# Mixer loop: decay sums placed between the outputs in both directions, step sizes computed inside the wait for the sums of squares, normalization scaled during the states

## The chip, the cores and the metric

The program runs on one core of a Trainium2 chip. The metric is device time in microseconds (us) of one execution; the kernel before has a median of 1464.55 us over three runs (1463.51 to 1469.52). A core has a matrix engine (PE), which also loads weights (PEld), a vector engine (DVE), an activation engine (ACT), a general engine (POOL) and a queue of DMA issues (SP). Each engine works through its own instructions in order; engines wait for each other by semaphores.

## The reference

Everything is float32. A batch of 8 images of 32x32 positions and 128 channels is read as 8 sequences of 1024 tokens. Layer 0 adds an attention over the tokens. Layer 1 adds a mixer, which is a state-space model run once forwards and once backwards over the tokens, and then adds a spectral filter. Only the mixer is touched by the change. Cut to its core it is:

```python
def mamba(x, in_proj, conv_w, conv_b, A_log, dt_bias, D, norm_w, out_proj):
    z, xbc, dt = split(x @ in_proj)                  # 256, 256 + 64 + 64, 4 columns
    xbc = silu(causal_conv(xbc, conv_w) + conv_b)    # 4 taps along the tokens
    xh, Bm, Cm = split(xbc)
    dt = softplus(dt + dt_bias)                      # one step size for token and head
    dA = dt * -exp(A_log)
    # per chunk of 64 tokens, cs = cumsum(dA)
    L = exp(cs_l - cs_s) for s <= l                  # decays inside the chunk
    y_in = (Cm @ Bm.T * L) @ (xh * dt)
    states = Bm.T @ (exp(cs_last - cs) * xh * dt)    # one state for a chunk and head
    prev = scan(states, exp(cs_last))                # 15 steps from chunk to chunk
    y = y_in + (Cm @ prev) * exp(cs) + xh * D
    y = y * silu(z)
    return (y * rsqrt(mean(y * y) + 1e-5) * norm_w) @ out_proj
t = layer_norm(x)
x = x + mamba(t, forward weights) + reverse(mamba(reverse(t), backward weights))
```

## The kernel before

The attention runs first, to about 456 us. The mixer follows, to about 1057 us, and the spectral filter takes the rest. The mixer has 16 units, one for each sequence and direction (`Unit(b, d)`, with d = 0 forwards and d = 1 backwards), in the order (0,0), (0,1), (1,0) and so on. One pass of the loop at L1258 finishes the recurrence of unit `u`, prepares the one after it (`following`) and closes the one before it (`last`). So three units are in flight. The order of instructions on every engine, SP included, is the order in which the Python code issues them (`manual_schedule(engines=ALL_IN_ORDER)`, L1220); nothing reorders them later. `behind(t, other)` adds a dependency by hand.

In what follows a forward pass is a pass whose `u` has d = 0, and a backward pass one whose `u` has d = 1. A forward pass also brings the tokens of the next sequence in (`fresh`): `turn_tokens` transposes them, `steps` makes the step sizes. A backward pass also normalizes the sequence after that (`normalize`, `normalized`).

What the steps do, with their tiles:

- `add_decays(u)` (L853): PE multiplies `da` with triangles into the PSUM tile `pdec`, ACT copies two results out (`cums`, `dsum`). `turn_decays(u)` (L868): one PE transpose of `cums` into the same `pdec`, one ACT copy (`cs`). `take_decays(u)` (L874): ACT takes exponentials (`cums`, `rest`, `dec`), SP stores them and loads them back spread over partitions (`lm`, `ec`).
- `from_row` (L903): POOL computes `cs - lm`, held `behind` the second convolution tap. `between` (L913): ACT applies Relu, and one pass later Exp, to the two halves of `lm`. `weigh_decays` (L1101): DVE multiplies `lm` by the products of B and C (`gm`, half of the tile `bg`).
- `project_x`, `copy_x`, `first_tap`, `convolve`, `activate_x`: projection (`pp`), copy (`xp`), first tap on ACT (`xs`, L954), three taps for each of two halves on DVE (L962), Silu on ACT (L967). `project_z` and `activate_z`: the gate (`pz`, `zs`, L975). `project_bc` and `activate_bc`: B and C (`pb`, then `bt` and `ct`, L1000).
- `turn_x` (L1005): 16 transposes on PE (`sx`), times the step size on DVE (`xdt`, L1016). `turn_b`: `sb`, copied by ACT to `bg` (L1038). `weigh_start` (L918): POOL multiplies `ec` by `ct`, held behind the last tap.
- `chunk_states` (`pst`) on PE, `pass_states` (L1080, L1083) on DVE, whose results SP copies to the other partitions (`moved`). `outputs` (`sy`, L1131): 248 small products in two halves.
- `end(last)` (L1228): the output projection `spo` and the sums of squares (`misc`, L1174), which ACT copies out (L1182), PE transposes (L1188), DVE scales (`rms_v`, L1190) and POOL raises to the power -0.5 (`rms`, L1192). `scale_rows` (L1196) multiplies `spo` by it on ACT; `add_rows` (L1202) adds to `X` on DVE.
- `steps` (L478): 8 small products (`pd`), three DVE instructions (`sp_v`, `sp_e`), Exp on ACT, one on DVE (`sp_u`), Ln on ACT, four on DVE. It is a generator, which the loop advances from `yield` to `yield`.
- `rsqrt` (L129): a POOL multiply-add (`ln_r_v`) and a POOL power (`ln_r`). In the mixer it is held behind the second tap.

PSUM has two pools here, each with two slots of 128x1024: `ps_w` (`sx`, `sb`, `px`, `pp`, `pd`, `pz`, `pb`, `pdec`) and `ps_s` (`spo`, `misc`, `pst`, `sy`). A tile gets a slot when the last reader of an earlier tile is done with it. In one pass `ps_s` is used in the order `spo`, `misc`, `pst`, `pst`, `sy`, `sy`; so the first `pst` waits for `scale_rows`, the last reader of `spo`.

Of the kernel before, what the change touches and what calls it, by code (L numbers as in the profile page):

```python
# [45 lines left out]
def fast_kernel(ctx: ExitStack, tc: tile.TileContext, a: dict, out: bass.AP, bad: bass.AP):  # L46
# [80 lines left out]
    begun = []  # L127

    def rsqrt(pool, src, n, scale, eps, name):  # L129

        t = pool.tile([P, n], F32, tag=name + "_v", name=name + "_v")
        begun.append(nc.gpsimd.tensor_scalar(t, src, scale, eps, ALU.mult, ALU.add))
        r = pool.tile([P, n], F32, tag=name, name=name)
        nc.gpsimd.tensor_tensor(r, t, mhalf.to_broadcast([P, n]), ALU.pow)
        return r
# [308 lines left out]
    def normalize(pool, b, later=False):  # L444
        st = pool.tile([P, NT, 6], F32, tag="ln_st", name=f"b_st{b}")
        mv = pool.tile([P, NT, 2], F32, tag="ln_mv", name=f"b_mv{b}")
        for j in range(NT):
            nc.vector.bn_stats(st[:, j, :], X[b][:, j, :])  # L448
        for j in range(NT):
            nc.vector.bn_aggr(mv[:, j, :], st[:, j, :])  # L450
        return mv, None if later else rsqrt(pool, mv[:, :, 1], NT, 1.0, 1e-5, "ln_r")
# [26 lines left out]
    def steps(b, seq, pd):  # L478
# [13 lines left out]
        for j in range(NT):  # L492
            nc.tensor.matmul(
                pd[:, j, :],
                lhsT=xt[:, pad + j * P : pad + (j + 1) * P],
                rhs=wdt.rearrange("p d h -> p (d h)"),
                start=True,
                stop=True,
            )
        v = small("sp_v")  # L500
# [3 lines left out]
        nc.vector.tensor_tensor(e, e, v, ALU.min)  # L504
        nc.scalar.activation(e, e, AF.Exp)
# [81 lines left out]
    with ExitStack() as s:  # L587
# [182 lines left out]
        for n in range(len(units) + 2):  # L770
# [35 lines left out]
            elif n == 117:  # L806
                sizes = steps(0, seqs[0], ps_t.tile([P, T], F32, tag="t", name="pd0"))
                next(sizes)
# [12 lines left out]
    with ExitStack() as s:  # L821
# [91 lines left out]
        def between(u, function, scale):  # L913

            for half in u.lm.rearrange("p (i h) j l -> i p (h j l)", i=2):
# [312 lines left out]
        def end(u, pool):  # L1228
# [5 lines left out]
            project_out(u, range(4, 6))  # L1234
            turn_sums(u, misc)
            project_out(u, range(6, 8))
# [9 lines left out]
        turn_decays(units[1])  # L1246
# [11 lines left out]
        for at, u in enumerate(units[:-1]):  # L1258
# [4 lines left out]
            early_decays = after_it and u.d == 1  # L1263
            if u.d == 1:
                turn_decays(following)
# [3 lines left out]
            between(u, AF.Exp, -1.0)  # L1269
# [5 lines left out]
            if fresh:  # L1275
                turn_tokens(fresh, seqs[fresh], wide_psum(ps_w, f"px{fresh}"))
            project_x(following, 0)
# [6 lines left out]
            if early_decays:  # L1284
                add_decays(after_it)
            causal(u)
            decayed_x(u)
            weigh_decays(u, 0)
            if last:
                end(last, ps_s)  # L1290
            if early_decays:
                turn_decays(after_it)
            first_tap(following, 0)
            if last:
# [4 lines left out]
            if u.d == 1 or u.b == B - 1:  # L1299
                norm = normalize(bridge, b, later=True)  # L1300
            going = iter(())
            if fresh:
                going = steps(fresh, seqs[fresh], wide_psum(ps_w, f"pd{fresh}"))
                next(going)
            weigh_decays(u, 1)
            convolve(following, 0, range(pad - 1))
            next(going, None)
# [4 lines left out]
            if norm:  # L1312
                mv = norm[0]
                norm = mv, rsqrt(bridge, mv[:, :, 1], NT, 1.0, 1e-5, "ln_r")
                behind(begun[-1], following.convolved, "beside the states")
            from_row(following, following.convolved)
            chunk_states(u)
            pass_states(u)
            next(going, None)
            norming = normalized(b, bridge, *norm) if u.d else iter(())  # L1320
            next(norming, None)
# [5 lines left out]
            between(following, AF.Relu, 1.0)  # L1327
# [4 lines left out]
            if after_it and not early_decays:  # L1332
                add_decays(after_it)
            activate_x(following, 1)
            next(norming, None)
# [1104 lines left out]
```

## Time and profile before

| | us |
|---|---|
| median of three runs | 1464.55 |
| the profiled execution | 1462.86 |
| its span, first to last instruction | 1461.1 |
| mixer, first `sx` of the first unit to first `sx` of the last | 533.4 |
| a forward pass, first `xdt` to first `xdt` of the next pass, as from 835.05 to 872.77 | 37.7 |
| a backward pass, as from 872.77 to 906.97 | 34.2 |

The times of a pass are read from the timeline of DVE: the first product with the step sizes (`xdt`, L1016) opens a pass, since it follows the first eight transposes. A row of the timeline gives the start, the duration, engine, line, operation and tiles (out<-in); in brackets stands how long the engine was idle before, and what released it. A row of the waits gives who waited for whom, the total in us, how often, and the longest. "issue" is a wait for which the profile shows no instruction.

### The profile page before, as it was taken

How to read it: one execution, taken by the hardware profiler on the slowest of the kernel's cores; microseconds unless marked ns; L12 is line 12 of the kernel's file. 1: busy time of each engine (PE TensorE's matmuls, PEld its weight loads, DVE VectorE, ACT ScalarE, POOL GpSimd, SP SyncE). 2: the span in 40 equal slices, each digit the busy share in tenths (PEclk: the TensorE clock that was granted, in tenths of full speed). 3: DMA queues.
4: the chain of work that ended last, by engine and by line, in shares of the span. 5: the costliest groups of instructions: out<-in, count | busy, mean ns of one | idle time of the engine just before them, and what ended most of it. 6: DMA issues, size and time to landing. Idle time of an engine off the chain costs nothing. (4 is left out here: it accounts for less than half of the span.)

```text
span 1461.1 us, 45273 instructions
## 1 busy us (share of the span) xinstructions
PE 1336.9 (91%) x19782; PEld 838.2 (57%) x19782; DVE 1094.3 (75%) x2138; ACT 912.1 (62%) x1421; POOL 504.1 (34%) x510
## 2 busy tenths in 40 slices
PE   5999999999998888999898898999789899999977
PEld 2223333333333566666666565656679899999963
DVE  5689889788777687878787878788555577777745
ACT  2666666766766777777777777776355455555520
POOL 3326966885400332323232323233276111111100
PEclk9999999999999999999999999999889999999989
DMA  7101111110002333433433343443269322322258
GB/s 181 36 1 30 45 37 37 42 46 23 8 1 59 73 74 86 91 88 88 89 88 88 89 90 86 100 92 71 73 193 240 110 69 78 85 69 76 69 147 322
DMA packets 139382, 123.09 MB, mean 84 GB/s; under 512 B 44808, under 2 KB 118152, under 8 KB 135080
## 3 DMA queue, kind: packets, MB, share of 16 engines
q1 hardware_dynamic: 137064, 115.93, 31.1%
q8 instruction: 157, 2.57, 0.8%
q10 hardware_dynamic: 2112, 4.19, 0.8%
q14 instruction: 49, 0.40, 0.1%
HBM read 78.15 MB, written 34.08 MB: 77 GB/s over the span
## 5 line engine op out<-in xcount | busy, mean ns | idle before, releaser
L692 ACT ACTIVATE pr<-pt 128x1024 f32<-128x1024 f32 x256 | 248.1, 1021 | 115.6 <-PE pt L687 114.1
L717 DVE TENSOR_TENSOR two<-pr,pr 128x1024 f32<-128x1024 f32 x128 | 162.8, 1312 | 19.8 <-ACT pr L692 18.9
L1514 ACT COPY gs<-pg 128x512 f32<-128x512 f32 x256 | 132.6, 603 | 63.8 <-PE pg L1501 47.9
L1512 DVE COPY gs<-pg 128x512 f32<-128x512 f32 x256 | 158.7, 682 | 14.6 <-PE pg L1501 9.6
L687 PE MATMUL pt<-q,k 32*128 32x512 f32 x1024 | 159.0, 650 | 7.0 <-ACT pr L692 4.7
L1501 PE MATMUL pg<-taps,mst 32*128 32x128 f32 x4096 | 146.0, 281 | 4.2 <-ACT gs L1514 3.4
L1501 PEld LDWEIGHTS pg<-taps,mst 32*128 32x128 f32 x4096 | 134.0, 189 | 16.4 <-issue 11.6
L708 PE MATMUL po<-pr,v 128*32 128x512 f32 x1024 | 141.2, 607 | 0.0
L1535 PE MATMUL py<-gs,u 128*32 128x128 f32 (+1 forms) x4096 | 127.8, 277 | 0.0
L984 PE MATMUL pb<-bxt,wbc 128*128 128x512 f32 x256 | 113.9, 597 | 14.5 <-ACT zs L975 14.5
L962 DVE SCALAR_TENSOR_TENSOR xs<-xp,cw,xs 128x1024 f32<-128x1024 f32 x96 | 121.8, 1282 | 4.7 <-issue 2.9
L920 POOL TENSOR_TENSOR ec<-ec,ct 128x2048 f32<-128x2048 f32 x16 | 72.6, 4536 | 144.0 <-ACT ct L1000 135.7
L1535 PEld LDWEIGHTS py<-gs,u 128*32 128x32 f32 (+1 forms) x4096 | 112.0, 141 | 7.2
L1524 POOL TENSOR_SCALAR u<-u 128x512 f32<-128x512 f32 x16 | 23.9, 1494 | 226.6 <-DMA u<-ud 126.4
L687 PEld LDWEIGHTS pt<-q,k 32*128 32x128 f32 x1024 | 47.0, 185 | 85.5 <-issue 31.3
L984 PEld LDWEIGHTS pb<-bxt,wbc 128*128 128x128 f32 x256 | 47.1, 189 | 71.8 <-issue 57.8
L1083 DVE SCALAR_TENSOR_TENSOR state<-state,dec,pst 128x64 f32<-128x64 f32 x448 | 87.4, 274 | 1.1
L1192 POOL TENSOR_TENSOR rms<-rms_v,mhalf 128x8 f32<-128x8 f32 x16 | 26.2, 1636 | 169.8 <-DVE rms_v L1190 169.8
L708 PEld LDWEIGHTS po<-pr,v 128*32 128x32 f32 x1024 | 27.6, 110 | 89.1 <-issue 84.8
L907 POOL TENSOR_TENSOR lm<-cs,lm 128x2048 f32<-128x2048 f32 x16 | 57.9, 3619 | 58.3 <-DVE sp_u L508 30.8
L1016 DVE TENSOR_TENSOR xdt<-sx,dt 128x1024 f32<-128x1024 f32 x32 | 37.8, 1220 | 52.3 <-PE sx L1013 52.3
L728 PE MATMUL pd<-two,ones 128*32 128x512 f32 x512 | 74.4, 612 | 0.2
(280 smaller groups left out, 2787.4 us busy)
## 6 DMA issues: line engine op xcount, KB each, us to landing
lm<-cd SPq DMA_DIRECT2D x32, 512.0 KB
ec<-cd SPq DMA_DIRECT2D x32, 512.0 KB
ud<-sp SPq DMA_DIRECT2D x8, 1024.0 KB
u<-ud SPq DMA_DIRECT2D x32, 256.0 KB
yd<-sums SPq DMA_DIRECT2D x32, 256.0 KB
moved<-state SPq DMA_DIRECT2D x48, 128.0 KB
yt<-yd SPq DMA_DIRECT2D x6, 1024.0 KB
X<-in_x SPq DMA_DIRECT2D x8, 512.0 KB
```

Source lines behind the costliest of these rows:

```text
L687: nc.tensor.matmul(pt[:, i, :], lhsT=k[rows, j * P : (j + 1) * P], rhs=q[rows, cols], start=True, stop=True)
L692: nc.scalar.activation(pr[:, 2 * g : 2 * g + 2, :].rearrange("p i t -> p (i t)"), pt.rearrange("p i t -> p (i t)"), AF.Exp, scale=SCALE,)
L708: nc.tensor.matmul(po[rows, :], lhsT=vs[b][:, j, rows], rhs=pr[:, h, :], start=(j == 0), stop=(j == NT - 1))
L717: nc.vector.tensor_tensor(two, sums["pr"][:, 2 * g : 2 * g + 2, :], pr[:, 2 * g : 2 * g + 2, :], ALU.add)
L728: nc.tensor.matmul(sums["d"][(2 * g + i) * DH : (2 * g + i + 1) * DH, :], lhsT=ones[:, :DH], rhs=two[:, i, :], start=(j == 1), stop=(j == ...
L962: u.convolved = nc.vector.scalar_tensor_tensor(acc, xp[:, at : at + T], cw[u.d][:, n, i : i + 1], acc, ALU.mult, ALU.add)
L984: nc.tensor.matmul(u.pb[:, i * 512 : (i + 1) * 512], lhsT=wbc[u.d][:, k, :], rhs=xt[:, at : at + 512], start=(k == 0), stop=(k == KC - 1),)
L1083: nc.vector.scalar_tensor_tensor(u.state[:, k, h, :], u.state[:, k - 1, h, :], u.dec[:, c, h, j : j + 1], u.pst[c][:, j, h, :], ALU.mult, ...
L1501: nc.tensor.matmul(pts[g][:, e, :], lhsT=mst[rows, n * 4 + e, :], rhs=taps[rows, cols].rearrange("p f q m i -> p (f q m i)"), start=True, ...
L1512: nc.vector.tensor_copy(to, frm)
L1514: nc.scalar.copy(to, frm)
L1535: nc.tensor.matmul(py[t * 32 : t * 32 + 32 - 16 * m, q // 2, :], lhsT=u[:, i, m:, :, :, q * FC + f].rearrange("p k b i -> p (k b i)"), rhs ...
```

## The change

Five things change in the loop over the units.

- `add_decays` of the unit after next is issued between the two halves of `outputs` in both directions. Before, a backward pass issued it after `project_x`, and `turn_decays` after `end`. Now every pass turns the decays of `following` at its start, and `turn_decays(units[1])` ahead of the loop is gone.
- `steps` has two more `yield`s. Its products are issued inside `end(last)`, in place of two of the eight rows of the output projection, which move behind the transposes of the sums. The Exp, and then the Ln, are issued ahead of `scale_rows`.
- The Exp over `lm` is split: the first half stays where both were, the second goes behind `turn_b` and `turn_tokens`.
- `rsqrt` of the normalization is issued right after the statistics, with no dependency added, and all eight scalings on ACT follow `from_row`. Before, four stood behind `pass_states` and four between the outputs.
- Relu over `lm` follows them, ahead of `chunk_states`. Before, it stood behind `activate_x(following, 0)`.

```diff
@@ -124,12 +124,10 @@
     mhalf = filled("mhalf", [P, 1], -0.5)
     quarter = filled("quarter", [P, 1], 0.25)
 
-    begun = []
-
     def rsqrt(pool, src, n, scale, eps, name):
 
         t = pool.tile([P, n], F32, tag=name + "_v", name=name + "_v")
-        begun.append(nc.gpsimd.tensor_scalar(t, src, scale, eps, ALU.mult, ALU.add))
+        nc.gpsimd.tensor_scalar(t, src, scale, eps, ALU.mult, ALU.add)
         r = pool.tile([P, n], F32, tag=name, name=name)
         nc.gpsimd.tensor_tensor(r, t, mhalf.to_broadcast([P, n]), ALU.pow)
         return r
@@ -441,14 +439,14 @@
         nc.vector.tensor_reduce(far[0:1, 0:1], pf, AX.X, ALU.add)
         nc.vector.tensor_copy(bad, far[0:1, 0:1])
 
-    def normalize(pool, b, later=False):
+    def normalize(pool, b):
         st = pool.tile([P, NT, 6], F32, tag="ln_st", name=f"b_st{b}")
         mv = pool.tile([P, NT, 2], F32, tag="ln_mv", name=f"b_mv{b}")
         for j in range(NT):
             nc.vector.bn_stats(st[:, j, :], X[b][:, j, :])
         for j in range(NT):
             nc.vector.bn_aggr(mv[:, j, :], st[:, j, :])
-        return mv, None if later else rsqrt(pool, mv[:, :, 1], NT, 1.0, 1e-5, "ln_r")
+        return mv, rsqrt(pool, mv[:, :, 1], NT, 1.0, 1e-5, "ln_r")
 
     def normalized(b, pool, mv, rstd, wide=None):
         shift = pool.tile([P, NT], F32, tag="ln_s", name=f"b_shift{b}")
@@ -497,11 +495,13 @@
                 start=True,
                 stop=True,
             )
+        yield
         v = small("sp_v")
         nc.vector.tensor_tensor(v, pd, wide(dtb), ALU.add)
         e = small("sp_e")
         nc.vector.tensor_scalar(e, v, -1.0, None, ALU.mult)
         nc.vector.tensor_tensor(e, e, v, ALU.min)
+        yield
         nc.scalar.activation(e, e, AF.Exp)
         yield
         u = small("sp_u")
@@ -805,7 +805,8 @@
                 turn_tokens(0, seqs[0], ps_t.tile([P, T], F32, tag="t", name="px0"))
             elif n == 117:
                 sizes = steps(0, seqs[0], ps_t.tile([P, T], F32, tag="t", name="pd0"))
-                next(sizes)
+                for _ in range(3):
+                    next(sizes)
             elif n in (121, 123):
                 next(sizes, None)
         assert not [*mixing, *making, *going, *coming]
@@ -910,9 +911,10 @@
             if other:
                 behind(t, other, "beside the states")
 
-        def between(u, function, scale):
-
-            for half in u.lm.rearrange("p (i h) j l -> i p (h j l)", i=2):
+        def between(u, function, scale, halves=(0, 1)):
+
+            for i in halves:
+                half = u.lm[:, 2 * i : 2 * i + 2].rearrange("p h j l -> p (h j l)")
                 nc.scalar.activation(half, half, function, scale=scale)
 
         def weigh_start(u, other):
@@ -1225,15 +1227,19 @@
             copy_x(u, n)
             first_tap(u, n)
 
-        def end(u, pool):
+        def end(u, pool, waiting=None):
 
             u.po = wide_psum(pool, f"spo{u.tag}").rearrange("p (j e) -> p j e", j=NT)
             project_out(u, range(4))
             misc = wide_psum(pool, f"misc{u.tag}")
             square_sums(u, misc)
-            project_out(u, range(4, 6))
+
+            if waiting:
+                waiting()
+            else:
+                project_out(u, range(4, 6))
             turn_sums(u, misc)
-            project_out(u, range(6, 8))
+            project_out(u, range(4 if waiting else 6, 8))
 
         add_decays(first)
         turn_decays(first)
@@ -1243,7 +1249,6 @@
         for n in range(2):
             take_x(first, n)
         add_decays(units[1])
-        turn_decays(units[1])
         convolve(first, 0)
         activate_x(first, 0)
         project(B - 1, 1, av, wide_psum(ps_w, "last_py")[:, :512].rearrange("p (i c) -> p i c", i=4))
@@ -1260,13 +1265,11 @@
             after_it = units[at + 2] if at + 2 < len(units) else None
 
             fresh = u.b + 1 if u.d == 0 and u.b + 1 < B else 0
-            early_decays = after_it and u.d == 1
-            if u.d == 1:
-                turn_decays(following)
+            turn_decays(following)
             if at == 0:
                 between(u, AF.Relu, 1.0)
             take_decays(following)
-            between(u, AF.Exp, -1.0)
+            between(u, AF.Exp, -1.0, (0,))
             turn_x(u)
             weigh_start(u, u.convolved)
             if last:
@@ -1274,6 +1277,7 @@
             turn_b(u)
             if fresh:
                 turn_tokens(fresh, seqs[fresh], wide_psum(ps_w, f"px{fresh}"))
+            between(u, AF.Exp, -1.0, (1,))
             project_x(following, 0)
             copy_x(following, 0)
             if last:
@@ -1281,58 +1285,52 @@
                 gate(last, 1)
             project_x(following, 1)
             copy_x(following, 1)
-            if early_decays:
-                add_decays(after_it)
             causal(u)
             decayed_x(u)
             weigh_decays(u, 0)
+            going = iter(())
+            if fresh:
+                going = steps(fresh, seqs[fresh], wide_psum(ps_w, f"pd{fresh}"))
             if last:
-                end(last, ps_s)
-            if early_decays:
-                turn_decays(after_it)
+                end(last, ps_s, (lambda: next(going)) if fresh else None)
+            elif fresh:
+                next(going)
+            next(going, None)
+            next(going, None)
             first_tap(following, 0)
+            next(going, None)
             if last:
                 scale_rows(last)
 
             b = (u.b + 2) % B
             norm = None
             if u.d == 1 or u.b == B - 1:
-                norm = normalize(bridge, b, later=True)
-            going = iter(())
-            if fresh:
-                going = steps(fresh, seqs[fresh], wide_psum(ps_w, f"pd{fresh}"))
-                next(going)
+                norm = normalize(bridge, b)
             weigh_decays(u, 1)
             convolve(following, 0, range(pad - 1))
-            next(going, None)
             for n in range(2):
                 project_z(u, n)
                 activate_z(u, n)
             first_tap(following, 1)
-            if norm:
-                mv = norm[0]
-                norm = mv, rsqrt(bridge, mv[:, :, 1], NT, 1.0, 1e-5, "ln_r")
-                behind(begun[-1], following.convolved, "beside the states")
             from_row(following, following.convolved)
+            for _ in normalized(b, bridge, *norm) if u.d else ():
+                pass
+            between(following, AF.Relu, 1.0)
             chunk_states(u)
             pass_states(u)
             next(going, None)
-            norming = normalized(b, bridge, *norm) if u.d else iter(())
-            next(norming, None)
             if stored:
                 reload(stored)
             stored = None
             convolve(following, 0, range(pad - 1, pad))
             activate_x(following, 0)
-            between(following, AF.Relu, 1.0)
             project_bc(following)
             activate_bc(following)
             convolve(following, 1)
             outputs(u, 0)
-            if after_it and not early_decays:
+            if after_it:
                 add_decays(after_it)
             activate_x(following, 1)
-            next(norming, None)
             outputs(u, 1)
             if last:
                 add_rows(last)
```

## The prediction

> **What bounds the kernel now.** I read the page first: PE is busy for most of the span, but that is an average.
>
> ```profile
> span 1461.1 us, 45273 instructions
> PE 1336.9 (91%) x19782; PEld 838.2 (57%) x19782; DVE 1094.3 (75%) x2138; ACT 912.1 (62%) x1421; POOL 504.1 (34%) x510
> ```
>
> Next I cut the mixer into passes: start, end, length, then busy time of PE, PEld, DVE, ACT and POOL. Here are one forward pass and the backward pass after it. PE idles for 5.1 and 3.6 us, and no other engine is full.
>
> ```profile
> 832.10:870.80 38.70, 33.59 (x515) 23.19 (x507) 28.45 (x58) 29.03 (x47) 10.44 (x8) 1.00 0.33 72
> 870.80:905.50 34.70, 31.08 (x484) 20.55 (x483) 29.03 (x67) 26.12 (x43) 11.76 (x8) 1.00 0.45 105
> ```
>
> Who makes PE wait? The waits from 545 to 943 us (11 passes) name ACT three times, and one wait with no cause:
>
> ```profile
> PE pb L984 <- ACT zs L975: 12.2, 11, 1.7
> ...
> PE sy L1131 <- issue: 8.9, 6, 2.2
> ...
> PE pp L929 <- ACT bg L1038: 6.5, 5, 1.3
> ...
> PE sx L1013 <- ACT xs L967: 6.0, 8, 1.6
> ```
>
> So I read ACT's timeline through that pair of passes, in the order in which ACT does it:
>
> ```profile
> 847.57 1.24 ACT L954 ACTIVATE xs<-xp,cb,cw 128x1024 f32<-128x1024 f32 x1
> 850.56 2.17 ACT L1200 ACTIVATE y<-spo,rms 128x128 f32<-128x128 f32 x8 [1.75 <-POOL rms L1192]
> 852.57 0.30 ACT L505 ACTIVATE sp_e<-sp_e 128x64 f32<-128x64 f32 x1
> 852.90 1.28 ACT L510 ACT_TABLE_LOAD   x1
> 855.66 0.26 ACT L510 ACTIVATE sp_l<-sp_u 128x64 f32<-128x64 f32 x1 [1.48 <-DVE sp_u L508]
> 855.93 1.28 ACT L975 ACT_TABLE_LOAD   x1
> 857.23 1.94 ACT L975 ACTIVATE zs<-pz 128x1024 f32<-128x1024 f32 x2
> ...
> 864.59 1.06 ACT L967 ACTIVATE xs<-xs 128x1024 f32<-128x1024 f32 x1 [4.30 <-DVE xs L962]
> 865.55 1.99 ACT L916 ACTIVATE lm<-lm 128x1024 f32<-128x1024 f32 x2
> 867.45 1.36 ACT L1000 ACTIVATE bt<-pb,cb 64x512 f32<-64x512 f32 x2
> ...
> 870.64 1.06 ACT L967 ACTIVATE xs<-xs 128x1024 f32<-128x1024 f32 x1
> ...
> 900.17 1.99 ACT L916 ACTIVATE lm<-lm 128x1024 f32<-128x1024 f32 x2
> ...
> 905.80 1.63 ACT L460 ACTIVATE ln_x<-X,b_shift,ln_r 128x128 f32<-128x128 f32 x4
> ```
>
> Two knots. At the end of each pass ACT is idle until DVE's third tap is done, then runs Silu, Relu, `bt`, `ct` and the second Silu without a gap, and the next pass opens when that ends. In a forward pass `zs` comes late, behind Ln and two table loads, and `pb` waits for it.
>
> **What the skill says.** "ScalarE: Activation LUTs", section "What ACT_TABLE_LOAD costs", puts 1.28 us on a load and 1.38 on a drain. Here the load takes 1.28 and the next instruction starts 0.02 later (855.93 + 1.28, then 857.23): no drain, so I count 1.3. "Runtime: NRT & Kernel Launch", section "Instruction fetch mechanics", says that instructions come in blocks of 16 KiB, 256 each, over a DMA queue. The trace agrees (queue q8: 157 transfers, 2.57 MB), and the "issue" waits in `sy` stand beside such transfers. "SBUF — State Buffer", section "SBUF: two separate sides", says that POOL and a DVE instruction with two SBUF inputs exclude each other. The trace agrees in the attention: a DVE sum of two tiles (L717), 1.2 us alone, takes up to 7.43 beside POOL, and the small power of L134 goes from 1.64 to 2.49.
>
> **The change, forward pass** (835.05 to 872.77, 37.7 us from `xdt` to `xdt`).
> 1. Start. Four of the eight `ln_x` (1.63) and one of two Exp over `lm` (1.0) leave the place ahead of the `bg` copy. Now `bg` starts at 839.68; it could at the end of `sb`, 838.42. Gain 1.2, all of the `pp` wait but 0.1. `pp` starts at 839.55. The second Exp fits where ACT waits for `pp` (1.16 idle before 842.77). Moving `pdec` costs nothing here.
> 2. End of `last`. PE does the same work: `spo` 1.95, `misc` 1.07, then `pd` 1.85 instead of two rows of `spo` (1.16), the transposes 0.38 and the rest of `spo`. So the transposes end at 848.1, and `pz` runs from 849.85 to 853.5.
> 3. DVE: `rms_v` at 848.25, then `sp_v` and two `sp_e` (0.7) to 849.1. ACT's Exp is queued ahead of the first tap, so ACT idles from 846.5 to 849.1 where it ran the tap before: Exp to 849.45, tap to 850.6, table to 851.9, Ln to 852.2, `scale_rows` to 854.35, table to 855.65, `zs` to 856.6. POOL's `rms` (1.63, to 850.1) is ready. `pb` starts at 856.65 instead of 858.30.
> 4. What is late next: `scale_rows` now ends 0.85 after `pz`, and it frees the slot of `pst`. So `pst` runs from 854.4 to 856.4. From there DVE needs what it needs now, `pst`'s end at 856.57 to the last tap at 868.39, so 11.8: 868.2.
> 5. End. Relu (2.0) moves to about 858.85, where ACT is idle until 864.59. Silu to 865.5, `bt` and `ct` 2.75 to 868.25, `cums` and `dsum` 0.45, second Silu to 869.8. `sy`, from 863.8 with its 5.0 to 5.3, ends before that. The next `xdt` follows the Silu by 1.08 as now (871.69 to 872.77): 870.85. The pass takes 35.8, a gain of 1.9.
>
> **Backward pass** (872.77 to 906.97, 34.2).
> 1. `pdec` and its transpose (0.41 + 0.41 + 0.61 + 0.24, overlapping, 1.2 on PE) leave the place ahead of `spo`. `spo` must still wait for the gate on DVE, 880.02, so 0.65 is won. The transposes of the sums end at 884.5, `rms` at 886.5, `scale_rows` at 888.7, `zs` at 890.95; `pb` starts at 891.05 instead of 892.04.
> 2. `ln_r` runs on POOL from 887 beside `weigh_decays` and two taps, which have two SBUF inputs each. It can be held up by one or two of them, to 890.8 or 892.0; DVE's `b_shift`, behind the taps at 890.7, waits for it, and the states behind it. I take 0; the other end is 1.2, which still lies under PE's end.
> 3. ACT: eight `ln_x` (3.28) to 896.4, Relu to 898.4 (`from_row` ends at 894.4), Silu to 899.45, `bt` and `ct` to 902.2, copies to 902.65, second Silu to 903.7, instead of 905.90.
> 4. PE is now the bound: `sy` starts at 898.1. From first to last start `sy` took 4.83 to 6.86 in the backward passes from 583 us on, mean 5.92, of which about 1.8 is the "issue" wait; forward passes, with `pdec` in the middle, took 5.0 to 5.6. If the 1.1 of `pdec` runs while the block comes, `sy` takes 5.9, and the next `xdt`, about 1.3 after the last start, comes at 905.3, in 32.5. If it adds in full, 33.6. ACT alone would allow 32.0. I take 33.0, a gain of 1.2.
>
> **The first and the last passes.** Ahead of the loop `pdec` of unit (0,1) now keeps one of the two `ps_w` slots until the first pass turns it. So `last_py`, `pb` and `pf` share the other one, and PE, in order, holds `sx` back behind `pf` until `ct` is out: by the same reckoning `pp` of the first pass comes 1.0 late instead of 1.0 early. Its `zs` then wins 2.0. Gain 1.0, bounds -1 and +3. Unit (0,1): 1.2. Unit (7,0) has no `steps` and loses Relu from its end: 1.1. The last unit's order stays.
>
> **Sum.** 1.0 + 1.2 + 6 x (1.9 + 1.2) + 1.1 = 21.9. The profiled execution took 1462.86 (span 1461.1), so 1441.0; the median stands 1.7 above it: 1442.6. The same gain falls on both, since nothing outside the mixer changes.
>
> **Rivals.** (a) Half the gain, 1452. Either DVE's `sp_e` is held off by the power `rms`, which starts at the same moment (1.4 later at Exp, at `scale_rows`, at `pst`; forward gain 0.5, total 21.9 - 7 x 1.4 = 12.1), or blocks of instructions come too late for a denser `sy` (backward gain 0.1, forward 0.3 less, total 12.1). For it: both resources are seen to stall. Against: the small powers at 124 and 175 us leave the DVE instruction beside them at 1.2. (b) Slower, 1475 to 1488. Today `ct` is out 1.8 after the last tap; afterwards both end at 868.2. So POOL's `ec` (4.53) and DVE's `add_rows` (L1204, two SBUF inputs) start together. If POOL wins, `add_rows` waits for 4.5 and the `xdt` behind it starts 3.2 late: 7 forward passes cancel the gain, 15 passes give +48 - 22. It decides when `ec` starts before L1204. Against: L1204 follows the tap on its own engine with no gap (863.28 + 5.11, start 868.31), POOL starts 0.08 after its releaser. (c) No measurable change: ACT's tail isn't what sets the pass. Against: the 4.30 idle, then no gap up to `sx`. (d) More, under 1436: backward passes reach ACT's 32.0.
>
> **From cases to numbers.** A change under 0.5%, 7.3 us, can't be told from none here. Forecast 0.62, (a) 0.22, (c) 0.06, (b) 0.06, (d) 0.04. So faster 0.88, same 0.06, slower 0.06. The range reaches down to backward passes at 32.0 (7 us) and up to case (a) with some pass on either side of it: 1436 to 1456.
>
> **What would show it.** Forward passes near 35.8 and backward ones near 33.0; `pp` waiting for `bg` gone in forward passes; `pb`'s wait in them shorter; `pst` waiting for `scale_rows` by about 0.9; ACT idle some 2.6 before L505; no Relu between the two Silu. The prediction is wrong if L1204 or `sp_e` stretch, if the issue waits in `sy` grow, or if the first pass is late by more than 2.

## The result, and the profile after

Measured beside the kernel before on one chip, the changed kernel takes 1451.65 us (median of four runs, 1449.31 to 1452.57), the kernel before 1464.12 (four runs, 1463.51 to 1469.52). The ratio is 0.9908, with a 95% interval of 0.9889 to 0.9926: faster by 0.9%, or 12.5 us, where 21.9 was forecast. The profiled execution took 1452.17, against 1462.86.

The head of the page of the kernel after, with the same two lines as before:

```profile
span 1450.4 us, 45285 instructions
PE 1341.4 (92%) x19782; PEld 842.2 (58%) x19782; DVE 1119.2 (77%) x2138; ACT 915.4 (63%) x1421; POOL 528.1 (36%) x510
```

The instructions of the engines are as many as before. Yet DVE is busy for 24.9 us more, and POOL for 24.0 more. Nothing in the change gives either engine more to compute: some instructions on each must have become longer. On POOL these are `ec` (10.8 in all) and the pair `ln_r_v` and `ln_r` (14.3).

Cut from `xdt` to `xdt`, the pair of passes that the prediction followed reads so (start, end, length, then busy time of PE, PEld, DVE, ACT and POOL, the clock, the DMA share and GB/s):

```profile
829.08:864.30 35.22, 33.90 (x509) 23.32 (x508) 28.44 (x58) 26.72 (x42) 10.70 (x8) 1.00 0.37 80
864.30:898.88 34.58, 31.27 (x485) 21.01 (x484) 32.44 (x68) 27.21 (x46) 14.37 (x8) 1.00 0.45 105
```

The forward pass takes 35.2 (before: 37.7; forecast: 35.8). The backward pass takes 34.6 (before: 34.2; forecast: 33.0): it got no shorter at all. DVE's extra time is in the backward pass: 32.44, where the prediction's cut of the kernel before has 29.03. In the forward pass it is 28.44, and was 28.45.

Who makes PE wait, over 11 passes (545 to 935 us), in the waits of the kernel after:

```profile
PE sy L1133 <- DVE state L1085: 7.5, 5, 1.5
PE sb L1032 <- DVE xdt L1018: 4.9, 11, 0.4
PE pb L986 <- ACT zs L977: 4.5, 11, 0.5
PE sy L1133 <- issue: 2.9, 3, 1.5
PE pst L1066 <- ACT y L1202: 2.8, 6, 0.7
```

The wait of `pp` for `bg` is gone, `pb` waits 4.5 instead of 12.2, the "issue" waits of `sy` fell from 8.9 to 2.9, and `pst` waits a little for `scale_rows` (0.5 a time, where about 0.9 was forecast). All of that was forecast, but for the fall of the "issue" waits, which the forecast left open. The first row was not: in each of the five backward passes of this window, the outputs wait 1.5 us for the states on DVE. Before, this wait does not appear.

The timeline of DVE of the kernel after, from 879 to 892, shows what made the states late (x28 stands for 28 steps one after the other):

```profile
879.14 2.61 DVE L964 SCALAR_TENSOR_TENSOR xs<-xp,cw,xs 128x1024 f32<-128x1024 f32 x2
881.96 3.58 DVE L453 SCALAR_TENSOR_TENSOR b_shift<-b_mv,ln_r 128x8 f32<-128x8 f32 x1 [0.21 <-POOL ln_r L132]
885.45 0.28 DVE L1082 COPY state<-pst 128x128 f32<-128x128 f32 x1
885.77 5.46 DVE L1085 SCALAR_TENSOR_TENSOR state<-state,dec,pst 128x64 f32<-128x64 f32 x28
```

`b_shift` reads eight numbers per partition and takes 3.58 us. The timeline of POOL at the same time:

```profile
879.37 2.56 POOL L132 TENSOR_TENSOR ln_r<-ln_r_v,mhalf 128x8 f32<-128x8 f32 x1
881.89 3.62 POOL L908 TENSOR_TENSOR lm<-cs,lm 128x2048 f32<-128x2048 f32 x1
...
896.48 5.31 POOL L922 TENSOR_TENSOR ec<-ec,ct 128x2048 f32<-128x2048 f32 x1 [10.97 <-ACT cums L864]
```

`ln_r` releases both engines at once. POOL has `from_row` next in its order and starts it at 881.89; DVE starts `b_shift` at 881.96, 0.07 later, and ends it at 885.54, with POOL's 885.51. The two instructions have two inputs each in SBUF, where the tiles of this kernel lie that aren't in a PSUM pool. In the kernel before, `from_row` ran from 893.03 beside the states, which read `pst` from PSUM and were not longer for it (5.46 both times), and `b_shift` came after both. The line of POOL and two of DVE:

```profile
893.03 3.62 POOL L907 TENSOR_TENSOR lm<-cs,lm 128x2048 f32<-128x2048 f32 x1
892.10 5.46 DVE L1083 SCALAR_TENSOR_TENSOR state<-state,dec,pst 128x64 f32<-128x64 f32 x28
897.47 0.16 DVE L455 SCALAR_TENSOR_TENSOR b_shift<-b_mv,ln_r 128x8 f32<-128x8 f32 x1
```

"SBUF — State Buffer" of the Trainium skill says in the section "SBUF: two separate sides" that such a pair of instructions, one on DVE and one on POOL, shares an exclusive lock: the one that starts first has it for the whole of its length. That fits: by this rule a lead of 0.07 us costs 3.4 us. (The last section has a POOL instruction that doesn't keep to it.) It also accounts for DVE's extra time: 7 backward passes times 3.4 are 24 us. So the theory is that the change pays for its gains with `b_shift`, in each of seven backward passes, since it put it right behind `from_row`. The rivals: PE had no more to give in a backward pass whatever DVE does (its "issue" waits would come instead), or ACT's longer row of `ln_x` and Relu sets the end, or the slot of `ps_w` kept by `pdec` of unit (0,1) costs the missing time at the start.

### The profile page after: what moved, and what is told of

Same layout as the page of the kernel before. It is cut to its first block, busy times and chain, and to the rows that moved or that the text cites. A ratio compares the mean times of both kernels' runs of the same rounds, so it can differ in the third digit from the quotient of the medians.

```text
span 1450.4 us, 45285 instructions
## 1 busy us (share of the span) xinstructions
PE 1341.4 (92%) x19782; PEld 842.2 (58%) x19782; DVE 1119.2 (77%) x2138; ACT 915.4 (63%) x1421; POOL 528.1 (36%) x510
## 5 line engine op out<-in xcount | busy, mean ns | idle before, releaser
L717 DVE TENSOR_TENSOR two<-pr,pr 128x1024 f32<-128x1024 f32 x128 | 163.4, 1317 | 21.4 <-ACT pr L692 20.5
L1499 PEld LDWEIGHTS pg<-taps,mst 32*128 32x128 f32 x4096 | 134.1, 190 | 16.7 <-issue 11.4
L922 POOL TENSOR_TENSOR ec<-ec,ct 128x2048 f32<-128x2048 f32 x16 | 83.4, 5212 | 163.9 <-ACT cums L864 143.0
L1133 PE MATMUL sy<-lm,xdt 64*64 64x64 f32 x2048 | 68.3, 224 | 17.5 <-DVE state L1085 10.5
L1133 PEld LDWEIGHTS sy<-lm,xdt 64*64 64x64 f32 x2048 | 61.3, 136 | 30.8 <-issue 28.1
```

Source lines behind the costliest of these rows:

```text
L717: nc.vector.tensor_tensor(two, sums["pr"][:, 2 * g : 2 * g + 2, :], pr[:, 2 * g : 2 * g + 2, :], ALU.add)
L1133: nc.tensor.matmul(u.py[c][h * HP : (h + 1) * HP, r, j, :], lhsT=left, rhs=right, start=(kind == 0), stop=(kind == 1 or k is None),)
L1499: nc.tensor.matmul(pts[g][:, e, :], lhsT=mst[rows, n * 4 + e, :], rhs=taps[rows, cols].rearrange("p f q m i -> p (f q m i)"), start=True, ...
```

## The experiments

**1. `from_row` behind `b_shift`.** On the changed kernel, backward passes only: DVE gets its small instruction first, and POOL waits for it.

```diff
-            from_row(following, following.convolved)
             for _ in normalized(b, bridge, *norm) if u.d else ():
                 pass
+            from_row(following, shifted[-1] if u.d else following.convolved)
```

`shifted` is a list to which `normalized` appends the instruction that writes `b_shift`.

> In backward passes POOL's from_row is held behind DVE's b_shift instead of behind the second tap; nothing else changes. Theory P (b_shift, with two SBUF inputs, is shut out for as long as from_row runs, 3.62 us): b_shift takes 0.16 instead of 3.58, the states start 3.4 us earlier, sy no longer waits 1.50 behind pb, backward passes go from about 34.5 to 33.0 and the whole to 1441 (1439 to 1445). Theory W (b_shift only waits for ln_r, whose end the profile shows too early): b_shift still takes over 3 us, from_row comes later by that, and the whole is 1452 or more.

It took 1437.79 (1437.07 to 1441.06), a ratio to the kernel before of 0.9809 (0.9773 to 0.9846). The timeline of DVE, and then that of POOL:

```profile
872.99 0.17 DVE L455 SCALAR_TENSOR_TENSOR b_shift<-b_mv,ln_r 128x8 f32<-128x8 f32 x1 [0.21 <-POOL ln_r L132]
873.19 0.29 DVE L1084 COPY state<-pst 128x128 f32<-128x128 f32 x1
```

```profile
870.40 2.56 POOL L132 TENSOR_TENSOR ln_r<-ln_r_v,mhalf 128x8 f32<-128x8 f32 x1
873.29 3.62 POOL L910 TENSOR_TENSOR lm<-cs,lm 128x2048 f32<-128x2048 f32 x1 [0.33 <-DVE b_shift L455]
```

`from_row` starts 0.33 after `ln_r`, `b_shift` takes 0.17, and the states follow at once. In the waits of PE there is no row of `sy` for the states any more; what is left of `sy` is

```profile
PE sy L1135 <- issue: 3.1, 6, 1.0
```

A backward pass takes 32.5 (mean of six) instead of 34.6, a forward pass 35.3 as in the changed kernel. This one order of two instructions is worth 13.9 us, more than the whole change gained. Of the 2.15 us of a pass, 1.55 is the start of `sy` (25.23 after the pass's `xdt` instead of 26.79), 0.4 is that `sy` lasts 5.8 instead of 6.2, and 0.2 the step from its last product to the next `xdt`. PE had more to give, so the first rival falls; ACT's `ln_x` and Relu were as long as in the changed kernel (3.18 and 2.00), so the second falls too. DVE's busy time over the whole is back at 1095.8. POOL's stays at 528.4, so what made `ec`, `ln_r_v` and `ln_r` longer isn't what held the backward pass up.

**2. The price of the pair by itself.** In the forward passes of the changed kernel, where nothing of the kind is, a small DVE instruction was put behind `from_row`, and its input, a fill on POOL, right ahead of it. One form has two inputs in SBUF, the other one. Nothing reads the result.

```diff
+            if not u.d:
+                probe = bridge.tile([P, 2, NT], F32, ...)
+                behind(nc.gpsimd.memset(probe[:, 0, :], 1.0), following.convolved, "probe")
             from_row(following, following.convolved)
+            if not u.d:
+                nc.vector.tensor_tensor(probe[:, 1, :], probe[:, 0, :], probe[:, 0, :], ALU.add)
```

The other form has `nc.vector.tensor_reduce(probe[:, 1, 0:1], probe[:, 0, :], AX.X, ALU.add)` in the last line.

> In forward passes, which have no b_shift, POOL writes a small tile ahead of from_row and DVE reads it, twice, in one added sum of 128x8 behind the taps, in the place that b_shift has in backward passes. Theory P: the added sum takes 2.5 to 3.6 us and ends when from_row ends; the states start about 1 us later, forward passes go from 35.2 to about 36, the whole to about 1458. Theory W: 0.2 us, no change.

> The same with a DVE reduction of the small tile, which has one SBUF input. Theory P: it takes about 0.2 us beside from_row, and the whole stays near 1452. Any other cause that sits in the wait for POOL's small instruction: as long as the sum with two inputs.

The groups by line of the two kernels (duration in ns, least, median and greatest), first that with two inputs, then that with one:

```profile
L1320 DVE TENSOR_TENSOR probe<-probe x8: 3566/3623/3625, 495.3 to 991.1; 128x8 f32<-128x8 f32 x8
```

```profile
L1320 DVE TENSOR_REDUCE probe<-probe x8: 160/161/163, 501.1 to 989.5; 128x1 f32<-128x8 f32 x8
```

With two inputs it takes as long as `from_row` does (3.62), in all eight places; with one, 0.16 beside the same `from_row`. Both start 0.02 to 0.07 after `from_row`. The two forms differ in the operation too, but the operation alone doesn't decide: `b_shift` and the steps of the states are the same one, and the steps, with one input in PSUM, kept their length. The forward pass grew from 35.3 to 36.2 in the one and stayed at 35.4 in the other. These are one profiled execution each (1458.54 and 1453.22), so the totals say little; the durations agree in all eight places.

**3. The normalization alone, on the kernel before.** `ln_r` right after the statistics, and all eight `ln_x` behind `from_row`; nothing else of the change.

```diff
-                norm = normalize(bridge, b, later=True)
+                norm = normalize(bridge, b)
...
             from_row(following, following.convolved)
+            for _ in normalized(b, bridge, *norm) if u.d else ():
+                pass
...
-            next(norming, None)
```

> The kernel before with the normalization part of the change alone: rsqrt at once, b_shift and all eight ln_x behind from_row. Theory P: b_shift takes 2.5 to 3.6 us beside from_row, the states come 2.7 us later and backward passes go from 34.2 to about 37; forward passes lose four ln_x ahead of the bg copy and go from 37.7 to about 36.5; 7 x (2.8 - 1.2) is 11 more than before, so about 1475. Theory W, or no shared port: backward passes stay at 34 or fall, and the whole is 1455 or less.

1481.49 (1479.03 to 1486.25), ratio 1.0128 (1.0104 to 1.0153): slower than the kernel before, by 17 us. `b_shift` in five backward passes, from its answer by tile:

```profile
L455 DVE SCALAR_TENSOR_TENSOR b_shift<-b_mv,ln_r x5: 3571/3572/3575, 606.2 to 902.2; 128x8 f32<-128x8 f32 x5
```

So this part of the change brings the stretch by itself; in experiment 5, without it, `b_shift` takes 0.16. Backward passes grow from 34.4 to 37.1, and `sx` waits 9.9 for ACT's last Silu, where it waited 6.0: here DVE's late taps also push the row of Silu, Relu, `bt`, `ct` and Silu, whose end comes 35.7 after `xdt` instead of 33.1. Forward passes win 0.7, since four of the `ln_x` have left their start.

**4. Relu back in its old place**, behind `activate_x(following, 0)`, in the changed kernel:

```diff
-            between(following, AF.Relu, 1.0)
             chunk_states(u)
...
             activate_x(following, 0)
+            between(following, AF.Relu, 1.0)
             project_bc(following)
```

> The changed kernel with Relu back behind activate_x(following, 0). If the end of each pass is ACT's run of Silu, Relu, bt, ct, Silu: forward passes +1.9 (to 37.2), backward passes +1.9 (to 36.5), the whole about 1478, slower than before. If Relu was hidden: 1452.

1482.42 (1480.99 to 1484.51), ratio 1.0132 (1.0115 to 1.0149). Forward passes are 2.1 and backward ones 2.2 longer than in the changed kernel (37.4 and 36.8): the 2.0 of Relu and a little. Two rows of the waits of PE show it, and two rows of its timeline show where:

```profile
PE pdec L871 <- ACT dsum L866: 10.5, 10, 1.5
PE sx L1015 <- ACT xs L969: 5.8, 10, 0.6
...
885.47 0.24 PE L871 MATMUL pdec<-ident,cums 32*128 32x32 f32 x1 [1.25 <-ACT dsum L866]
...
886.55 2.90 PE L1015 MATMUL sx<-ident,xs 128*128 128x128 f32 x15 [0.58 <-ACT xs L969]
```

L871 is `turn_decays` at the head of the next pass. It needs ACT's copies of the sums, which stand behind `ct`, and `sx` right after it needs the second Silu. With Relu ahead of all of them, PE has done its outputs and stands still twice, until ACT's row is at its end. In the changed kernel the same transpose waits for 0.2 in all in these passes. What the new place of the sums would cost beside Relu in its old one can't be told apart here: the second Silu ends after the copies in any case.

**5. Relu alone, on the kernel before**, moved to the place right behind `from_row`:

```diff
             from_row(following, following.convolved)
+            between(following, AF.Relu, 1.0)
...
-            between(following, AF.Relu, 1.0)
             project_bc(following)
```

> The kernel before with one edit: the Relu over lm right behind from_row, off the row of ScalarE's work at a pass's end. If that row of Silu, Relu, bt, ct and Silu sets the end of every pass of the kernel before: 15 passes times 2.0, 1434, which is all that the change is worth in its best form, and the other moves carry nothing. If TensorE takes over as the bound (its idle in a pass is 3.7 us forward and 3.2 backward, and part of it lies ahead of the outputs): about half, 1449.

1451.21 (1448.89 to 1454.89), ratio 0.9905 (0.9875 to 0.9935). That is the whole gain of the change, with one line moved. In the profiled execution, the slowest of its five (1454.89), forward passes take 36.2 instead of 37.5, backward passes 34.8 instead of 34.4. The waits of PE:

```profile
PE pb L984 <- ACT zs L975: 12.2, 11, 1.7
PE sy L1131 <- issue: 9.6, 7, 2.5
...
PE pp L929 <- ACT bg L1038: 2.6, 2, 1.3
```

The waits of `sx` for ACT's last Silu are down from 6.0 to 1.2, but those of `sy` for instructions are not. With ACT out of the way, a backward pass meets PE, and gains nothing on average: all start `sy` at 26.3 after `xdt`, and those with a `sy` of 4.5 to 5.1 us take 33.2, those with one of 7 take 35.3 to 35.5.

**6. The sums of decays where they were**, in the kernel of experiment 1 (so that `b_shift` doesn't cover the difference): backward passes issue them ahead of `causal` again, and turn them behind `end`; those of unit (0,1) are turned ahead of the loop.

```diff
         add_decays(units[1])
+        turn_decays(units[1])
...
+            early_decays = after_it and u.d == 1
+            if u.d == 1:
+                turn_decays(following)
-            turn_decays(following)
...
+            if early_decays:
+                add_decays(after_it)
             causal(u)
...
+            if early_decays:
+                turn_decays(after_it)
...
-            if after_it:
+            if after_it and not early_decays:
                 add_decays(after_it)
```

> The changed kernel with from_row behind b_shift (its first edit alone gave 1437.8), and with the sums of decays where they stood before: every second unit's in the head of a backward pass ahead of causal, turned behind end. If they cost what the prediction reckoned for the head (pb 0.65 to 1.0 later) and the outputs win nothing back: a backward pass of 33.1 to 33.5 instead of 32.5, a forward pass as it is, and 1442 to 1445. If TensorE is so full in these passes that it is all the same where its work stands: 1438.

1441.66 (1437.02 to 1443.21), ratio 0.9838 (0.9794 to 0.9881). The interval overlaps with that of experiment 1, so the totals don't settle it. The passes of the two profiled executions speak for a small cost: the backward ones take 33.4 instead of 32.5, the forward ones stay at 35.4. `pb` ends 26.38 after `xdt` instead of 25.30, so 1.1 later, and its wait isn't longer. `sy` wins next to nothing back: from first to last start it takes 5.7 on average, against 5.8 with 1.1 us of `pdec` in its middle. The waits say why:

```profile
PE sy L1135 <- issue: 7.5, 4, 2.2
```

Without `pdec` between them, PE waits up to 2.2 us for instructions among the outputs; with it, 1.0 at most.

The traces also show what PE waits for there. The prediction took these waits for late blocks of instructions, and the transfers of queue q8, which brings them, agree: in the traces of the 14 kernels here, each of the 93 "issue" waits of over 0.3 us in `sy` ends 2.2 to 3.1 us after the last transfer of this queue has started (median 2.4), though these transfers are 9.4 us apart on average. In experiment 6 that transfer starts 0.0 to 0.9 us before PE stands still, in experiment 1 it starts 1.4 to 2.3 before: PE does `pdec` while the block comes.

**7. The turned decays of unit (0,1) ahead of the loop again**, which frees the slot of `ps_w`:

```diff
         add_decays(units[1])
+        turn_decays(units[1])
...
+            if at:
-            turn_decays(following)
+                turn_decays(following)
```

> turn_decays of unit (0,1) is put back ahead of the loop; nothing else changes. If the slot that pdec keeps is what holds pf and the first sx back: pf no longer waits 2.86 us for ct, the first xdt comes some 4 us sooner after the first pdec (24.3 us now, 19.7 before), of which the first pass gives back part, so 1449 (1447.5 to 1450.5). If not: 1451.6.

1451.69 (1447.07 to 1454.79), ratio 0.9896 (0.9855 to 0.9937): no difference from the changed kernel, where 1449 was expected. The first `xdt` of the mixer does come earlier, 20.15 after the first `pdec` instead of 24.32. But the first pass then takes 34.97 instead of 31.29. The sum differs by 0.5 us.

**8. `scale_rows` ahead of the Ln**, against the wait of `pst`:

```diff
-            next(going, None)
             if last:
                 scale_rows(last)
+            next(going, None)
```

> The changed kernel with scale_rows issued ahead of sp_u and Ln. If the end of scale_rows is what holds the first pst (0.46 us in forward passes): that wait is gone, zs stays where it is, the states start 0.5 to 0.8 us earlier, and forward passes, which PE then sets alone, fall by 0.1 to 0.4: 1450 (1448.5 to 1451.5). If Ln's place matters for zs instead: pb later, 1453.

1452.38 (1452.22 to 1455.58), ratio 0.9929 (0.9912 to 0.9945). `pst` waits no more, and `pb` takes the wait over, which in the changed kernel was 4.5 in all and 0.5 at most:

```profile
PE pb L986 <- ACT zs L977: 9.8, 11, 1.5
```

The forward pass is 35.2 as before the edit. The same 0.9 is waited for at one place or the other, since ACT still has Ln and its table load ahead of `zs`. The 1450 that was expected isn't reached.

**9. The step sizes in their old place**, behind `normalize`, with no wait inside `end`:

```diff
-                end(last, ps_s, (lambda: next(going)) if fresh else None)
-            elif fresh:
-                next(going)
-            next(going, None)
-            next(going, None)
+                end(last, ps_s)
             first_tap(following, 0)
-            next(going, None)
...
                 norm = normalize(bridge, b)
+            for _ in range(3):
+                next(going, None)
             weigh_decays(u, 1)
             convolve(following, 0, range(pad - 1))
+            next(going, None)
```

> The changed kernel with steps where the kernel before had it: products behind the whole output projection, Exp and Ln behind scale_rows and the taps. By my reckoning zs comes 0.45 us later and pst does not wait: forward passes go from 35.3 to about 35.7, the whole to about 1454.5. If the steps were the larger part of the gain: 36.5 or more, 1460.

1450.84 (1446.89 to 1456.07), ratio 0.9924 (0.9898 to 0.9949). Forward passes take 35.7 instead of 35.3. The wait of `pb` is back (1.73 in a forward pass instead of 0.37) and that of `pst` (0.46) is gone. In the total, 0.4 in seven forward passes can't be seen.

**10. Both halves of the Exp ahead of `bg`**, as before:

```diff
-            between(u, AF.Exp, -1.0, (0,))
+            between(u, AF.Exp, -1.0)
...
-            between(u, AF.Exp, -1.0, (1,))
```

> The changed kernel with both halves of the Exp issued ahead of bg again, as before; everything else as changed. If the split of the Exp is what brought bg forward and took the wait of pp away (prediction's forward step on bg, 1.2 us earlier): the wait of pp comes back, a forward pass is near 36.3 instead of 35.2 and the whole 1459. If ScalarE has spare time ahead of bg since ln_x no longer stands there (it is idle 1.24 us before bg in the changed kernel's forward pass): no change, 1452.

1456.1 (1449.14 to 1459.84), ratio 0.9922 (0.9893 to 0.9952). Forward passes are 35.4 and `pp` doesn't wait for `bg` in them. So the split carries nothing that these runs can tell from none: with four of the `ln_x` gone from this place, ACT is idle for 1.24 us ahead of `bg` in the changed kernel, and the second Exp (1.06) fits there.

**11. Experiments 1, 7 and 8 together.**

> The changed kernel with three edits at once: from_row behind b_shift in the backward passes (worth 13.9 us alone), the turned decays of unit (0,1) ahead of the loop (0 alone) and scale_rows ahead of the step that issues sp_u and the Ln (0 alone). If b_shift is the one thing that the change paid for and the other two only move TensorE's idle time from one wait to another: 1438, within 2 us of the first edit alone, with the backward pass near 32.5 and the forward pass near 35.2. If the two others were hidden by the b_shift wait behind them: 1434 or less.

1434.2 (1431.21 to 1435.55), ratio 0.9778 (0.9751 to 0.9806): the fastest of all the kernels here, by 2.2% against the kernel before. Its passes, 35.2 and 32.5, are close to those of experiment 1 (35.3 and 32.5). Of the 7.0 us by which its profiled span is shorter, 4.9 lie ahead of the mixer, in code that is the same in both; the mixer is 2.3 shorter, nearly all of it before the end of the first pass. The intervals of the two ratios overlap, so whether it beats experiment 1 is open; that both beat the changed kernel is not.

## Why the prediction was right or wrong

The direction, the range (1436 to 1456) and the forecast forward pass held; the size was 12.5 instead of 21.9. That the range held is in part luck: it reached up to 1456 for case (a), whose causes did not come, and the loss in the backward passes has another cause. The profiled executions show where the rest is. In us gained, by place:

| | forecast | measured, before and after |
|---|---|---|
| start of the mixer | 0 | -1.3 (457.49, 458.79) |
| from there to the end of the first pass | 1.0 | 0.1 (19.69 + 36.03, 24.32 + 31.29) |
| unit (0,1) | 1.2 | -0.5 (34.20, 34.68) |
| six forward passes | 11.4 | 13.3 (37.51, 35.30 each) |
| six backward passes | 7.2 | -1.4 (34.40, 34.63 each) |
| unit (7,0) | 1.1 | 1.4 (32.88, 31.44) |
| last unit, to its last `spo` | 0 | 1.2 (42.76, 41.56) |
| after the mixer | 0 | -2.2 (406.62, 408.81) |
| sum | 21.9 | 10.6 |

The first and the last but one row have nothing to do with the edits: the mixer of experiment 1 begins at 460.2, that of experiment 11 at 455.3, and what lies after the mixer is 408.8 in experiment 3 too, whose code there is that of before.

**Forward steps 1 to 5: right.** The wait of `pp` is gone. Only the wait of `pst` came to half of its forecast (0.5 instead of 0.9). From the timeline of ACT in the kernel after:

```profile
832.48 1.01 ACT L1040 COPY bg<-sb 128x1024 f32<-128x1024 f32 x1 [1.24 <-PE sb L1032]
...
843.12 0.26 ACT L505 ACTIVATE sp_e<-sp_e 128x64 f32<-128x64 f32 x1 [2.64 <-DVE sp_e L503]
...
845.98 2.16 ACT L1202 ACTIVATE y<-spo,rms 128x128 f32<-128x128 f32 x8
...
849.45 1.94 ACT L977 ACTIVATE zs<-pz 128x1024 f32<-128x1024 f32 x2
...
852.41 2.00 ACT L918 ACTIVATE lm<-lm 128x1024 f32<-128x1024 f32 x2
...
862.17 1.06 ACT L969 ACTIVATE xs<-xs 128x1024 f32<-128x1024 f32 x1
```

ACT idles 2.64 ahead of the Exp of `sp_e` (forecast 2.6). `scale_rows` ends 19.06 after `xdt` (forecast 19.3), and the second Silu 34.15 after it (forecast 34.75). Each of the five steps came a little early, which makes 35.2 out of 35.8. The runs also tell the parts apart: Relu is worth 1.3 on the kernel before (experiment 5) and 2.1 on the changed one (4), the four `ln_x` 0.7 (3), the place of the step sizes 0.4 (9), the split of the Exp nothing (10). The parts lean on each other, so they don't simply add up to the 2.2.

**Backward step 1: right.** `pb` starts 18.19 after `xdt`; forecast 18.28.

**Backward step 2: the one that failed.** It said of `b_shift` and the states behind it: "I take 0; the other end is 1.2, which still lies under PE's end." `ln_r` was held up beside the taps as the step said (2.56, and `ln_r_v` 1.08 instead of 0.20), and ended 17.6 after `xdt`; 18.0 was forecast. But the step priced only the wait for `ln_r`. It had `from_row` end at 894.4 in the next step, so start at the moment at which it let `b_shift` start, and it had used the rule on two SBUF inputs for `ln_r` in the same step; it didn't ask what the same rule does to `b_shift`. The term that it took as 0, with 1.2 as the far end, came to 3.4: `b_shift` took 3.58 instead of 0.16. That doesn't lie under PE's end: `sy` starts 1.5 late. Experiments 1, 2 and 3 show it: with the overlap taken away the stretch is gone, with the overlap made elsewhere it is there, and with this part of the change alone the kernel is slower.

**Backward step 3: overtaken.** ACT's second Silu ended 33.4 after `xdt` instead of 30.9, as it followed the late taps (30.2 in experiment 1).

**Backward step 4: right, behind the failed one.** With `b_shift` out of the way, `sy` starts 25.23 after `xdt` (forecast 25.33), and PE sets the end. Of its two cases, `pdec` done while the block comes (32.5) and `pdec` added in full (33.6), the first is the measured one: 32.5, and the "issue" waits fell as `pdec` came between (experiment 6). The forecast of 33.0 between them gave 0.5 us a pass away.

**First pass: right in its mechanism, a wash in its size.** `pf` waits for `ct`, 2.9 us, as was said. Counted from the first `pdec`, the first `xdt` is 4.6 late, `pp` 1.65 (forecast 1.0), and `pb` is still 0.6 late, where 1.0 early was forecast; the pass ends 0.1 early. Experiment 7 takes the wait away and gets nothing: the time comes back in the same pass. So 0.1 instead of 1.0. The prediction called itself wrong if the first pass was late by more than 2; that holds for its start and not for its end.

**The rivals.** The measured time is that of (a), half the gain, but by neither of its two ways: `sp_e` was not held off by the power (0.20 and 0.23 us in the timeline of DVE), and the "issue" waits of `sy` became fewer. A right number from a wrong cause would have sent the next edit to the wrong place. The range of (b), 1475 to 1488, doesn't follow from its own terms, which give about 1465 (7 passes, 22.4 lost against 21.9 won) to 1491 (15 passes). (b) didn't come: `ec` started 0.3 after `add_rows` (896.48 and 896.17), and it was POOL that was held up, 5.31 instead of 4.53, while L1206 took its 1.22. (c) falls with experiments 4 and 5. (d), ACT's 32.0, was not reached; with experiment 1 the backward passes come to 32.5.

**One reading.** The 7.43 that the prediction gives for the sum of L717 beside POOL is the longest wait of DVE's queue on that line. The sum itself takes 3.39 at most, in the kernel before, beside a POOL sum that had started 1.0 ahead of it. This changes the figure and not the rule.

## What to carry to other kernels

When an instruction moves, look at what each other engine starts at the same time as it, not only at what it waits for: here a small DVE instruction with two SBUF inputs that became ready together with a long POOL one cost the length of the POOL one. Order the pair by hand, the short one first, and leave beside the long one what reads PSUM or has one SBUF input. And a gain in one place may pay for a loss in another: here one moved line was worth as much as the whole change, so a change of several parts is best measured part by part.

## What the runs showed of the hardware

- Two DVE instructions of 128x8 elements with two SBUF inputs took 3.57 to 3.62 us when they started 0.02 to 0.07 us after POOL's 128x2048 subtraction (3.62), and ended 0.02 after it. One of them, `b_shift`, takes 0.16 alone; the other ran only there. A reduction of 128x8, with one input, took 0.16 in the same place, and 28 steps of the states with one operand in PSUM took 5.46 with it and without it.
- It is not so for each POOL instruction: beside the power of 128x8 (`rms`, 1.63), DVE's sum of 128x64 with two SBUF inputs took 0.23. The sum started 0.3 after the power and ended with it still running, so the power doesn't hold such an instruction off for the whole of its length. The other way round, POOL's power takes 2.56 instead of 1.64 beside two taps that keep their 1.3 each.
- The "issue" waits of PE among 64x64 products depend on what stands between the products. In the kernel before they came to 8.9 in eleven passes: five waits of 0.7 to 2.2 in backward passes, which have nothing else there, and one of 0.3 in a forward pass, which has the sums. With 1.1 us of other work in the middle of every pass they came to 2.3 to 5.0, at most 1.7 (the changed kernel and experiments 1, 4 and 7 to 11); without it in backward passes to 7.5, at most 2.2 (experiment 6). They end 2.2 to 3.1 us after a transfer of the instruction queue has started.
